# Six shifted copies of a transformed row: twelve transfers inside SBUF in place of a store to DRAM and a load

## The chip, the cores and the metric

The kernel runs on one core of one Trainium2 chip. The metric is the device time of one execution in microseconds (us). Times of runs of one kernel differ by about 0.2%.

The engines are called as in the profile: PE is TensorE (matmuls; PEld is its loading of weights), DVE is VectorE, ACT is ScalarE, POOL is GpSimd, and SP is SyncE, which here only issues DMAs. All DMAs run on 16 DMA engines. SBUF is the on-chip memory with 128 partitions, PSUM the memory that matmuls write to, DRAM the memory off the core.

## The reference

The input x has the shape (4, 512, 512, 16): four images of 512 x 512 pixels with 16 channels, float32. Two layers follow one another, each added to its input after a group normalization `_gn`:

```python
x = x + _L0_conv_ref(_gn(x), h0, numerators, denumerator)
x = x + _L1_conv_ref(_gn(x), kernel, bias, radius)
```

The first layer is a convolution by way of Fourier transforms. A filter of 16 x 16 channels is given as a quotient of two polynomials in two dimensions:

```python
H_truncated = rfft2(b, s=(512, 512)) / rfft2(a, s=(512, 512))
h_truncated = irfft2(H_truncated, s=(512, 512))
H = rfft2(h_truncated, s=(1024, 1024))
H_full = h0 + H[0]
X = rfft2(x, s=(1024, 1024), axes=(-3, -2))
Y = einsum('...hwi,ijhw->...hwj', X, H_full)
y = irfft2(Y, s=(1024, 1024), axes=(-3, -2))
return y[..., :512, :512, :]
```

So at every frequency a vector of 16 input channels is multiplied by a 16 x 16 matrix, for each of the four images. The second layer is a 3 x 3 convolution with a normalization by the norm of the input window, an arc cosine and a gate; it isn't touched here.

## The kernel before

`body` runs four stages after one another. `filter_phase` makes the spectrum of the filter along one axis and stores it to DRAM as `g_d`. `forward_phase` transforms the normalized image along the same axis and stores it as `x_d`. `conv_phase` does the other axis and the product of the channels, and stores `y_d`. `last_phase` transforms back and does the second layer. The change touches `conv_phase` alone.

`conv_phase` runs over 513 rows (frequencies of the first axis; the first row of all is split in two planes). The second axis has 512 points, which the kernel treats as 8 blocks of 64 points, each transformed to 128 frequencies; the convolution over whole blocks is what the shifted slots below are for. A row n goes through these steps:

- `load_x(n)` and `load_g(n)` bring the row of the image (128 partitions x 2 KB) and of the filter (128 x 8 KB) into SBUF, on SP's DMA queue.
- `x_part(n, b)` multiplies the image row by a Fourier matrix on PE, and `evict` copies the result from PSUM to slot 0 of `xe`. A row's `xe` is a tile of 128 partitions x 8 slots x 1024 floats (4 KB a slot and partition), with three buffers. The partition stands for a pair of a block and a channel: 8 blocks x 16 channels. A shift by one block is a shift by 16 partitions.
- `x_late(n)` makes on POOL a second version `xl` of slot 0, multiplied by complex factors `late`: four products into the scratch tile `u` (named xu in the profile, L807), one product into `xl` (L808) and one addition (L809).
- Slots 1 to 7 of `xe` hold slot 0 shifted by 16, 32, up to 112 partitions. The partitions that would come from beyond the end come from `xl`, from its start.
  - Slot 4, the shift by 64, is made by two copies on ACT in `half_shift` (L818): partitions 64 to 127 of slot 0 go to partitions 0 to 63, and partitions 0 to 63 of `xl` go to partitions 64 to 127.
  - For the six others, `store(0, ...)` and `store(1, ...)` in `x_late` write slot 0 from partition 16 on, and `xl` up to partition 111, one below the other to a DRAM buffer `xf_d` (L800, issued on POOL's queue). Then `load_xe` (L824, on SP's queue) reads it back with overlapping rows: one transfer for slots 1 to 3 and one for slots 5 to 7, each with 128 partitions x 3 slots x 4 KB. There are four DRAM buffers, used in turn.
- `g_part(n, j)` turns the filter row into its spectrum `gh` on PE (L838), with evictions on ACT and DVE.
- `mix(n, g)` does the product over the channels (L854): for each of 128 frequencies one matmul of `gh` with all eight slots of `xe`. It is the only reader of the slots other than slot 0 (and, with the change, of slot 4 as scratch).
- `over_q` and `over_g` transform the result `yf` back along this axis (PE L875 and L912, ACT L882, DVE L883 to L887, POOL L891 and L893), and the row goes to `y_d` by a DMA on POOL's queue (L923).

`step(n)` sets the program's order: it does `mix` for row n, `g_part` for row n+1, `over_q` for row n-1, `x_part`, `x_late` and `half_shift` for row n+2, `over_g` for row n-2, in four parts k = 0 to 3. Before the parts it loads x of row n+3, g of row n+2, and the shifted slots of row n+1. A planner orders the instructions of each engine from this program before the kernel runs, by its own costs, and sets the waits; an engine then runs its instructions in that fixed order. In the trace the order on ACT within a row is: evictions of part 0, one eviction of xe, the first copy of `half_shift`, evictions of part 1, the second copy of `half_shift`, evictions of part 2 and 3. PSUM has three banks for `pg`, two for `pm`, and three that `px`, `pz` and `py` share.

Of the kernel before, what the change touches and what calls it, by code (L numbers as in the profile page):

```python
# [40 lines left out]
F32 = mybir.dt.float32  # L41
# [5 lines left out]
P = 128  # L47
N = 512
B = 4
C = 16  # L50
S = 64
F = 128
# [4 lines left out]
XF = F * 2 * B  # L57
# [144 lines left out]
def bc(ap, axis, shape):  # L202
    return ap.unsqueeze(axis).to_broadcast(shape)
# [501 lines left out]
def conv_phase(tc, cst, g_d, x_d, y_d):  # L705
    nc = tc.nc
    with ExitStack() as ctx:
# [3 lines left out]
        xlp = ctx.enter_context(tc.tile_pool(name="h_xl", bufs=1))  # L711
# [10 lines left out]
        ig = load_const(nc, cp, cst, "ig").rearrange("p (s c n) -> p s c n", s=4, c=2)  # L722
        late = load_const(nc, cp, cst, "late").rearrange("p (v f) -> p v f", v=3)

        xf_d = [tc.dram_tile([16 * C, XF], F32, name=f"xf_d{n}") for n in range(4)]


        rows = [(0, 0, 0), (0, 0, 1)] + [(n // P, n % P, None) for n in range(1, N)]
        n_rows = len(rows)
        state = {}  # L730
        flip = [0]

        def evict(dst, src):
            flip[0] += 1
            if flip[0] % 3 == 0:
                nc.vector.tensor_copy(dst, src)  # L736
            else:
                nc.scalar.copy(dst, src)  # L738

        def load_g(n):  # L740
            rc, r, plane = rows[n]
            g = io.tile([P, C, 8 * C], F32, name="g")
            t, w = g.rearrange("p j x -> p (j x)"), C * 8 * C
            if plane is None:
                nc.sync.dma_start(out=t, in_=dram(g_d[rc], r, 0, [w, P], [1, w]))
            else:
                for to, at in ((0, (0, 96)[plane]), (64, (64, 32)[plane])):
                    nc.sync.dma_start(out=t[to : to + 32], in_=dram(g_d[rc], r, at * w, [w, 32], [1, w]))
                    nc.gpsimd.memset(t[to + 32 : to + 64], 0.0)
            state["g", n] = g  # L750

        def load_x(n):
            rc, r, plane = rows[n]
            x = io.tile([P, B, 8 * C], F32, name="x")
            t, w = x.rearrange("p b x -> p (b x)"), B * 8 * C
            if plane is None:
                nc.sync.dma_start(out=t, in_=dram(x_d[rc], r, 0, [w, P], [1, w]))
            else:
                nc.gpsimd.memset(t[S:], 0.0)
                nc.sync.dma_start(out=t[:S], in_=dram(x_d[rc], r, plane * S * w, [w, S], [1, w]))  # L760
            state["x", n] = x
# [16 lines left out]
        def x_part(n, b):  # L778

            if b == 0:  # L780

                state["xe", n] = xep.tile([P, 8, F, 2, 2, 2], F32, name="xe")
            if b % 2 == 0:
                state["px"] = ps_f.tile([P, 2, F, 2], F32, name="px", tag="full")
            px = state["px"]
            nc.tensor.matmul(px[:, b % 2].rearrange("p f c -> p (f c)"), state["x", n][:, b],
                             state["dfs", n], start=True, stop=True)
            if b % 2:
                evict(state["xe", n][:, 0, :, b // 2], px.rearrange("p k f c -> p f c k"))
            if b == B - 1:  # L790
                del state["x", n], state["dfs", n]

        def x_late(n):

            xe = state["xe", n][:, 0]
            fl = xe.rearrange("p f h c k -> p f (h c k)")

            def store(half, t):
                at = slice(C, P) if half == 0 else slice(0, P - C)
                nc.gpsimd.dma_start(out=xf_d[n % 4][half * P :, :][at], in_=t[at].rearrange("p f x -> p (f x)"))  # L800

            store(0, fl)
            xl = xlp.tile([P, F, 2, 2, 2], F32, name="xl")
            u = xlp.tile([P, F, 2, 2, 2], F32, name="xu")
            for c in range(2):
                for h in range(2):
                    nc.gpsimd.tensor_mul(u[:, :, h, c], xe[:, :, h, 1 - c], bc(late[:, 1 + c], 2, [P, F, 2]))  # L807
            nc.gpsimd.tensor_mul(xl.rearrange("p f h c k -> p f (h c k)"), fl, bc(late[:, 0], 2, [P, F, 8]))  # L808
            nc.gpsimd.tensor_add(xl.rearrange("p f h c k -> p (f h c k)"),  # L809
                                 xl.rearrange("p f h c k -> p (f h c k)"),  # L810
                                 u.rearrange("p f h c k -> p (f h c k)"))
            store(1, xl.rearrange("p f h c k -> p f (h c k)"))
            state["xl"] = xl

        def half_shift(n, half):

            dst, src = ((slice(0, 64), state["xe", n][64:, 0]), (slice(64, P), state["xl"][:64]))[half]
            nc.scalar.copy(state["xe", n][dst, 4].rearrange("p f h c k -> p (f h c k)"),  # L818
                           src.rearrange("p f h c k -> p (f h c k)"))

        def load_xe(n):
            src = xf_d[n % 4]
            for t in (1, 5):
                nc.sync.dma_start(  # L824
                    out=state["xe", n][:, t : t + 3].rearrange("p t f h c k -> p t (f h c k)"),
                    in_=bass.AP(tensor=src.tensor, offset=src.offset + t * C * XF,
                                ap=[[XF, P], [C * XF, 3], [1, XF]]),
                )

        def g_part(n, j):  # L830


            if j % 4 == 0:
                state["pg"] = [ps_g.tile([P, 4, F], F32, name=f"pg{c}", tag="pg") for c in range(2)]
            g, pg = state["g", n], state["pg"]
            for c in range(2):
                half = slice(64 * c, 64 * c + 64)
                nc.tensor.matmul(pg[c][:, j % 4], g[half, j], dg[half], start=True, stop=True)  # L838
            if j == 3:
                state["gh", n] = ghp.tile([P, F, 2, C], F32, name="gh")  # L840
            if j % 4 == 3:
                for c in range(2):
                    evict(state["gh", n][:, :, c, j - 3 : j + 1], pg[c].rearrange("p j f -> p f j"))
            if j == C - 1:
                del state["g", n]

        def mix(n, g):

            if g % 8 == 0:
                state["pm"] = ps_m.tile([P, 8, 8, 2 * B], F32, name="pm")  # L850
            xe, gh, pm = state["xe", n], state["gh", n], state["pm"]
            for q in range(4):
                f = g + 32 * q
                nc.tensor.matmul(  # L854
                    pm[32 * q : 32 * q + 32, g % 8], gh[:, f].rearrange("p c j -> p (c j)"),
                    xe[:, :, f].rearrange("p t h c k -> p t (h c k)"), start=True, stop=True,
                )
            if g == 7:

                state["y", n] = yp.tile([P, 16, 32, 4], F32, name="yf")  # L860
            if g % 8 == 7:
                evict(state["y", n][:, :, g - 7 : g + 1].rearrange("p t g x -> p g t x"),
                      pm.rearrange("p g t (h x) -> p g (t h) x", h=2))
            if g == 31:
                del state["xe", n], state["gh", n]
# [65 lines left out]
        def step(n):  # L931


            def row(k):
                return 0 <= n + k < n_rows

            if row(3):
                load_x(n + 3)
            if row(2):
                load_g(n + 2)  # L940
            if row(1):
                load_xe(n + 1)
            for k in range(4):
                if row(0):
                    for g in range(8):
                        mix(n, 8 * k + g)
                if row(1):
                    for j in range(4):
                        g_part(n + 1, 4 * k + j)
                if row(-1):  # L950
                    for t in range(4):
                        over_q(n - 1, 4 * k + t)
                if row(2) and k == 0:
                    for m in range(B):
                        x_part(n + 2, m)
                    x_late(n + 2)
                if row(2) and k >= 2:
                    half_shift(n + 2, k - 2)
                if row(3) and k == 2:
                    turn_x(n + 3)  # L960
                if row(-2) and k == 2:
                    for m in range(4):
                        over_g(n - 2, m)

        for n in range(-3, n_rows + 2):
            step(n)
# [479 lines left out]
```

## Time and profile before

| what | value |
|---|---|
| median of the three runs | 18372.5 us |
| the runs | 18348.46, 18387.49, 18372.5 us |
| the profiled execution | 18378.82 us |
| its span (first to last instruction) | 18377.0 us |
| mean granted PE clock | 0.939 of full speed |
| first and last copy of `half_shift` | 6426.3 and 15491.8 us |
| HBM read and written | 3030.71 and 1477.31 MB |

The profile is one execution. Its span is cut into 40 slices of 459 us; the slices that carry a digit of the busy share show the stages. Groups of instructions are named by line, engine, output and input, with a count, the total busy time and the mean of one. A list of waits gives for each waiting line the line that released it, the total of idle time, how often, and the longest. A DMA share of 1 is all 16 DMA engines busy; it can come out a little above 1 in a short stretch. A name in the profile is a tile's name: xe, xl, xu, gh, pm and pg are those of the text above.

In the trace of one row (9003 to 9020 us), the products of row n+2 on POOL run from 9007.5 to 15.3 us past 9000, the two copies of `half_shift` on ACT start at 9008.75 and 9015.31, the store of `xl` is issued at 9015.57, and the loads of the slots are issued at 9019.54 and 9020.54.

### The profile page before, as it was taken

Reading aid. Unit: us, or ns where it says so; the run is one execution under the profiler, and the core shown is the slowest. Engines: PE = TensorE matmul, PEld = TensorE weight load, DVE = VectorE, ACT = ScalarE, POOL = GpSimd, SP = SyncE. Lnnn points to the kernel's source line nnn. Section 1 sums busy time; section 2 is a strip of 40 time slices with the busy share of each in tenths; the row PEclk is TensorE's granted clock in tenths of the full one; section 3 lists DMA queues with packets and bytes.
Section 4 is the critical chain, followed back from the end, with each engine's and each line's share of the span. In section 5 each row is a group of like instructions: output and inputs, shape, how many; then the busy total and the mean of one; then the engine's idle time right before and its main releaser. Section 6 shows DMA issues by size and latency. Waiting matters only on the chain. (4 is left out here: it accounts for less than half of the span.)

```text
span 18377.0 us, 546088 instructions
## 1 busy us (share of the span) xinstructions
PE 16100.0 (88%) x233100; PEld 11615.5 (63%) x233100; DVE 11247.9 (61%) x23131; ACT 9599.6 (52%) x19919; POOL 10502.4 (57%) x10653
## 2 busy tenths in 40 slices
PE   7788888888889988888888888888888988988888
PEld 4444444444444467777777777777767776877777
DVE  8877777777833355555555555555555554246887
ACT  4556555555632255555555555555555554106788
POOL 5566666666621166666666666666666664026776
PEclk6888988888999999999999999999999999998999
DMA  4655555555676588888888888888888887795431
GB/s 123 201 162 165 162 165 162 164 163 161 167 221 184 167 319 320 318 321 324 316 321 318 319 325 323 325 325 323 323 323 314 325 320 289 257 324 192 160 129 69
DMA packets 2918877, 4543.47 MB, mean 247 GB/s; under 512 B 117634, under 2 KB 2086492, under 8 KB 2809694
## 3 DMA queue, kind: packets, MB, share of 16 engines
q1 hardware_dynamic: 2686254, 3768.39, 60.7%
q0 software_dynamic: 174896, 605.89, 8.7%
q10 hardware_dynamic: 55296, 134.24, 2.2%
q8 instruction: 1835, 30.06, 0.6%
q14 instruction: 596, 4.88, 0.1%
HBM read 3030.71 MB, written 1477.31 MB: 245 GB/s over the span
## 5 line engine op out<-in xcount | busy, mean ns | idle before, releaser
L838 PE MATMUL pg<-c_dg,g 64*128 64x128 f32 x32832 | 2836.9, 291 | 326.6 <-ACT gh L738 163.0
L854 PE MATMUL pm<-xe,gh 128*32 128x64 f32 x131328 | 2397.8, 222 | 587.8 <-issue 354.6
L854 PEld LDWEIGHTS pm<-xe,gh 128*32 128x32 f32 x131328 | 2011.9, 110 | 1165.3 <-issue 972.6
L838 PEld LDWEIGHTS pg<-c_dg,g 64*128 64x128 f32 x32832 | 2283.3, 190 | 670.4 <-issue 253.4
L456 PE MATMUL pt<-ev_in,c_todd 128*128 128x512 f32 x4096 | 2191.1, 681 | 350.4 <-ACT ot L461 323.9
L883 DVE TENSOR_TENSOR z<-zq,pz 128x256 f32<-128x256 f32 x2052 | 861.4, 420 | 2608.4 <-ACT zq L882 2531.1
L736 DVE COPY gh<-pg 128x512 f32<-128x512 f32 x2046 | 1410.1, 689 | 1312.1 <-PE pg L838 1308.2
L379 POOL TENSOR_TENSOR x<-ab,ab 128x512 f32<-128x512 f32 x1024 | 1561.1, 1524 | 1081.7 <-ACT ab L362 1029.0
L807 POOL TENSOR_TENSOR xu<-xe,c_late 128x256 f32<-128x256 f32 x2052 | 1389.5, 702 | 860.2 <-ACT xe L738 834.6
L377 DVE RECIPROCAL dn<-dn 128x256 f32<-128x256 f32 x1024 | 1781.8, 1740 | 0.0
L456 PEld LDWEIGHTS pt<-ev_in,c_todd 128*128 128x128 f32 x4096 | 792.4, 210 | 1483.1 <-issue 640.1
L738 ACT COPY yf<-pm 128x512 f32<-128x512 f32 x2046 | 1210.9, 592 | 924.0 <-PE pm L854 909.2
L362 ACT COPY ab<-pab 128x512 f32<-128x512 f32 x2048 | 1127.9, 617 | 858.7 <-PE pab L353 609.1
L818 ACT COPY xe<-xl 64x1024 f32<-64x1024 f32 x513 | 538.5, 1050 | 1872.5 <-POOL xl L809 1872.5
L738 ACT COPY gh<-pg 128x512 f32<-128x512 f32 x2058 | 1200.0, 583 | 398.4 <-PE pg L838 389.5
L875 PE MATMUL pz<-c_ident,yf 128*128 128x128 f32 x8208 | 1377.4, 291 | 30.3 <-issue 28.5
L404 PE MATMUL pg<-c_dinv,sp 64*128 64x128 f32 x16384 | 1192.7, 301 | 117.8 <-ACT sp L393 117.8
L404 PEld LDWEIGHTS pg<-c_dinv,sp 64*128 64x128 f32 x16384 | 1084.7, 209 | 313.2 <-PE pab L353 134.1
L376 DVE TENSOR_TENSOR m<-ab,ab 128x512 f32<-128x512 f32 x1024 | 1271.4, 1242 | 0.0
L809 POOL TENSOR_TENSOR xl<-xl,xu 128x1024 f32<-128x1024 f32 x513 | 1208.9, 2357 | 40.2
L383 POOL TENSOR_TENSOR m<-m 128x256 f32<-128x256 f32 x1024 | 747.0, 730 | 746.4 <-DVE m L376 746.2
L1289 PE MATMUL pc<-l_band,xn 128*128 128x160 f32 (+2 forms) x6144 | 1072.9, 333 | 53.7 <-DVE e_o L1344 53.5
(204 smaller groups left out, 31381.8 us busy)
## 6 DMA issues: line engine op xcount, KB each, us to landing
xe<-xf_d SPq DMA_DIRECT2D x1026, 1536.0 KB, 8.4
g<-g_d SPq DMA_DIRECT2D x511, 1024.0 KB, 9.8
g_d<-st SPq DMA_DIRECT2D x64, 4096.0 KB, 31.3
ev_in<-g_d SPq DMA_DIRECT2D x1024, 256.0 KB, 4.6
g_d<-ot SPq DMA_DIRECT2D x1024, 256.0 KB, 2.5
xf_d<-xe POOLq DMA_DIRECT2D x513, 448.0 KB, 8.3
xf_d<-xl POOLq DMA_DIRECT2D x513, 448.0 KB, 5.2
x_d<-xo SPq DMA_DIRECT2D x128, 1024.0 KB, 5.1
```

The costliest lines, as they stand in the source:

```text
L376: nc.vector.tensor_mul(w["m"], b, a)
L377: nc.vector.reciprocal(w["dn"], w["dn"])
L379: nc.gpsimd.tensor_mul(w["x"], b, a[:, :, ::-1])
L404: nc.tensor.matmul(pg[u][:, n, k].rearrange("p a x -> p (a x)"), w["sp"][q, k, c, :], dinv[q, 2 * kp + k, c, :], start=(c == 0), stop=(c = ...
L456: nc.tensor.matmul(pt, todd[:, c, kc, hh * P : hh * P + P], ev[:, kc, c], start=(kc == 0), stop=(kc == 1),)
L736: nc.vector.tensor_copy(dst, src)
L738: nc.scalar.copy(dst, src)
L807: nc.gpsimd.tensor_mul(u[:, :, h, c], xe[:, :, h, 1 - c], bc(late[:, 1 + c], 2, [P, F, 2]))
L809: nc.gpsimd.tensor_add(xl.rearrange("p f h c k -> p (f h c k)"), xl.rearrange("p f h c k -> p (f h c k)"), u.rearrange("p f h c k -> p (f ...
L838: nc.tensor.matmul(pg[c][:, j % 4], g[half, j], dg[half], start=True, stop=True)
L854: nc.tensor.matmul(pm[32 * q : 32 * q + 32, g % 8], gh[:, f].rearrange("p c j -> p (c j)"), xe[:, :, f].rearrange("p t h c k -> p t (h c k ...
L875: nc.tensor.transpose(pz[:, t % 4].rearrange("p v q x -> p (v q x)"), y[:, at].rearrange("p g x -> p (g x)"), ident)
```

## The change

`xf_d`, both stores and `load_xe` are taken out. A new function `shift` copies, for each of the six slots, the part that comes from slot 0 (half 0) and the part that comes from `xl` (half 1), each with one DMA from SBUF to SBUF on SP's queue: twelve a row, of 112, 96, 80, 48, 32 and 16 partitions in half 0, and of 16, 32, 48, 80, 96 and 112 in half 1, with 4 KB a partition. They stand in the program right before and after `x_late`, for row n+2, one row earlier than `load_xe` stood. `xl` has two buffers in place of one, and the scratch `u` is now slot 4 of the row's own `xe`, which `half_shift` writes over later.

```diff
-        xf_d = [tc.dram_tile([16 * C, XF], F32, name=f"xf_d{n}") for n in range(4)]
-
...
             xe = state["xe", n][:, 0]
             fl = xe.rearrange("p f h c k -> p f (h c k)")
 
-            def store(half, t):
-                at = slice(C, P) if half == 0 else slice(0, P - C)
-                nc.gpsimd.dma_start(out=xf_d[n % 4][half * P :, :][at], in_=t[at].rearrange("p f x -> p (f x)"))
-
-            store(0, fl)
-            xl = xlp.tile([P, F, 2, 2, 2], F32, name="xl")
-            u = xlp.tile([P, F, 2, 2, 2], F32, name="xu")
+            xl = xlp.tile([P, F, 2, 2, 2], F32, name="xl", bufs=2)
+            u = state["xe", n][:, 4]
...
-            store(1, xl.rearrange("p f h c k -> p f (h c k)"))
             state["xl"] = xl
...
-        def load_xe(n):
-            src = xf_d[n % 4]
-            for t in (1, 5):
-                nc.sync.dma_start(
-                    out=state["xe", n][:, t : t + 3].rearrange("p t f h c k -> p t (f h c k)"),
-                    in_=bass.AP(tensor=src.tensor, offset=src.offset + t * C * XF,
-                                ap=[[XF, P], [C * XF, 3], [1, XF]]),
-                )
+        def shift(n, half):
+
+            xe, src = state["xe", n], state["xl"] if half else state["xe", n][:, 0]
+            for t in (1, 2, 3, 5, 6, 7):
+                at = C * t
+                to, of = ((slice(0, P - at), slice(at, P)), (slice(P - at, P), slice(0, at)))[half]
+                nc.sync.dma_start(out=xe[to, t].rearrange("p f h c k -> p f (h c k)"),
+                                  in_=src[of].rearrange("p f h c k -> p f (h c k)"))
...
-            if row(1):
-                load_xe(n + 1)
...
                 if row(2) and k == 0:
                     for m in range(B):
                         x_part(n + 2, m)
+                    shift(n + 2, 0)
                     x_late(n + 2)
+                    shift(n + 2, 1)
```

More of the change, by code (lines that the diff above doesn't have):

```diff
@@ L819, in half_shift @@
                            src.rearrange("p f h c k -> p (f h c k)"))
-        def load_xe(n):
-            src = xf_d[n % 4]
-            for t in (1, 5):
-                nc.sync.dma_start(
-                    out=state["xe", n][:, t : t + 3].rearrange("p t f h c k -> p t (f h c k)"),
-                    in_=bass.AP(tensor=src.tensor, offset=src.offset + t * C * XF,
-                                ap=[[XF, P], [C * XF, 3], [1, XF]]),
-                )
+        def shift(n, half):
[3 more added lines that the diff above has]
+                to, of = ((slice(0, P - at), slice(at, P)), (slice(P - at, P), slice(0, at)))[half]
+                nc.sync.dma_start(out=xe[to, t].rearrange("p f h c k -> p (f h c k)"),
+                                  in_=src[of].rearrange("p f h c k -> p (f h c k)"))
         def g_part(n, j):
```

## The prediction

> **What bounds the kernel now.** I began with the page's busy shares and slices, to find the stage that the change touches, went on to the table of DMA issues, then to the list of waits of PE inside that stage, then to stretches of one microsecond, and last to the order of instructions within one row.
>
> ```profile
> PE 16100.0 (88%) x233100; PEld 11615.5 (63%) x233100; DVE 11247.9 (61%) x23131; ACT 9599.6 (52%) x19919; POOL 10502.4 (57%) x10653
> DMA  4655555555676588888888888888888887795431
> GB/s 123 201 162 165 162 165 162 164 163 161 167 221 184 167 319 320 318 321 324 316 321 318 319 325 323 325 325 323 323 323 314 325 320 289 257 324 192 160 129 69
> ```
>
> The flat run of twenty slices at about 320 GB/s is conv_phase, from about 6420 to 15530 us. Nothing outside it changes. Per row it moves:
>
> ```profile
> xe<-xf_d SPq DMA_DIRECT2D x1026, 1536.0 KB, 8.4
> g<-g_d SPq DMA_DIRECT2D x511, 1024.0 KB, 9.8
> xf_d<-xe POOLq DMA_DIRECT2D x513, 448.0 KB, 8.3
> xf_d<-xl POOLq DMA_DIRECT2D x513, 448.0 KB, 5.2
> x<-x_d SPq DMA_DIRECT2D x511, 256.0 KB, 12.1
> y_d<-yo POOLq DMA_DIRECT2D x511, 256.0 KB, 3.1
> ```
>
> Two loads of 1536 KB, two stores of 448 KB, g, x and y make 3.146 + 0.918 + 1.049 + 0.262 + 0.262 = 5.64 MB. Between 7000 and 15000 us there are 452.5 copies of each half shift, so a row takes 8000/452.5 = 17.68 us, and 5.64 MB in that is 319 GB/s, as the page shows. The DMA share there is 0.865 (seven stretches of 460 us lie between 0.86 and 0.88): 15.3 us of all 16 engines in each 17.68.
>
> PE is busy 0.89 of the same time, so it idles 1.97 us a row. Its waits in that stretch (waiting line, what released it, us in total, times, longest):
>
> ```profile
> PE pm L854 <- issue: 308.6, 302, 4.6
> PE pg L838 <- ACT gh L738: 137.5, 165, 3.7
> PE pg L838 <- issue: 134.9, 90, 3.0
> PE pm L854 <- DMA xe<-xf_d: 90.4, 66, 3.2
> PE pm L854 <- ACT zq L882: 52.5, 144, 0.6
> ```
>
> "Issue" is the largest: with the smaller ones on py, pz and px 503 us, 1.11 us a row, idling inside groups of equal matmuls where no operand is awaited. The list of the first 6000 us, at a DMA share near 0.56, has no such entry for PE. Two of them (9042 and 9048 us) fall where the DMA share is 1.00 or more. I read them as instructions arriving late behind data on the DMA engines; that is an inference. Next come 0.42 us a row behind ACT and 0.20 behind a late xe load. So PE is the nominal bound, and DMA, almost full, is what delays it.
>
> Within a row the engines alternate between full and nearly empty (us, then busy time and count of PE, PEld, DVE, ACT, POOL, then PE clock, DMA share, GB/s):
>
> ```profile
> 9018.00:9019.00 1.00, 1.00 (x15) 0.88 (x12) 0.90 (x4) 1.00 (x3) 0.48 (x1) 1.00 0.44 156
> 9024.00:9025.00 1.00, 1.00 (x39) 0.67 (x41) 0.93 (x5) 0.32 (x1) 0.60 (x1) 1.00 1.08 442
> ```
> ```profile
> 6418.00:6419.00 1.00, 0.00 (x0) 0.00 (x0) 0.00 (x0) 0.00 (x0) 0.91 (x1) 0.50 0.78 156
> 6419.00:6420.00 1.00, 0.00 (x0) 0.00 (x0) 0.00 (x0) 0.00 (x0) 0.00 (x0) 0.50 0.94 273
> 6420.00:6421.00 1.00, 0.00 (x0) 0.00 (x0) 0.31 (x1) 0.51 (x1) 0.00 (x0) 0.50 0.68 234
> 6421.00:6422.00 1.00, 0.72 (x2) 0.67 (x3) 0.42 (x2) 0.51 (x1) 0.00 (x0) 0.50 0.89 238
> ```
>
> These give prices in engine-us per MB (share x 16 / MB moved in 1 us). Loads over 128 partitions, at 9024: 1.08 x 16 / 0.442 = 39. The tail of the store from xl, 112 partitions, at 9018: 0.44 x 16 / 0.156 = 45. From 6418 to 6422 mostly the first g and x loads, on 32 and 64 partitions, are in flight: 3.29 x 16 / 0.901 = 58.
>
> **What it removes.** Both stores (0.918 MB) and the DRAM side of the loads. POOL loses two issues of 0.57 and 0.58 us a row; it has idle time in every row (1.65 us ahead of xu alone, 741.7/452), so the issues count only where they delay xl:
>
> ```profile
> 9008.75 1.04 ACT L818 COPY xe<-xe 64x1024 f32<-64x1024 f32 x1 [1.35 <-DVE xe L736]
> 9008.96 0.57 POOL L800 DMA_DIRECT2D xf_d<-xe  x1
> ...
> 9012.92 2.36 POOL L809 TENSOR_TENSOR xl<-xl,xu 128x1024 f32<-128x1024 f32 x1
> ...
> 9015.31 1.05 ACT L818 COPY xe<-xl 64x1024 f32<-64x1024 f32 x1 [3.75 <-POOL xl L809]
> ```
>
> The first store stands between two pairs of xu; without it, xl is done 0.66 us sooner (the 8.85 to 9.55 gap, less the usual 0.04). SP's wait for the store from xl, 5809.5/452 = 12.9 us a row, goes, and with it the dip seen at 9018; SP's wait held back only the g load behind it. The late loads go if the copies land sooner: they are issued a row earlier, so -0.20 us a row, -103 us.
>
> **What it adds.** On SP twelve issues replace two: at the load's median of 0.39 us, 4.7 us instead of 0.8. SP idles 12.9 us a row there, so I cost this at nothing; the longest issue at that line was 3.2 us, and twelve such would not fit a row. The first six wait for DVE's eviction of xe, the last six for xl at about 9014.6; behind them on SP stand the next x and g loads. g cannot start before about 9019.5, when its buffer comes free, and x has more than a row, so nothing is late. If the six were delayed past that, g_part in the next row would be next to wait, since g takes 9.8 us to land.
>
> PE's first mix of a row must now see twelve transfers, not two. Its queue has two semaphore instructions there, at 51 ns least; ten more would be 0.5 us, under the 2.1 us that the second one waits anyway. Nothing, or +260 us without that cover. Similar waits of 17 to 49 ns on ACT, DVE and POOL lie in their idle time.
>
> u moves into slot 4 of xe: same shape, and slot 0 of the same buffer has to be free by then in any case. The second xl buffer removes waits that sum to 3.2 us in the whole run. Both nothing.
>
> **What it moves.** Slot 4 is now scratch until the add at L809 has read it, so the first half shift, at 9008.75 now, cannot run before about 9014.6. ACT then owes two copies of 1.05 us where one stood; if they go back to back, the eviction behind them comes 1.05 - 0.66 = 0.39 us later, at most +200 us; if the second copy goes after the evictions, they come 0.66 us sooner, at most the 0.42 us that PE waits for ACT, -215 us. The order isn't visible in this trace. I take +200 where DMA doesn't bind; where it does, the wait is hidden by that.
>
> **The term that decides: 3.146 MB from SBUF to SBUF.** No row shows one. Lower bound, as cheap as a full load: 39 x 3.146 / 16 = 7.7 us. Upper bound, a narrow load and a store one after the other: 58 + 45 = 103, 20.3 us. Nearer rows lie inside: the narrow loads (58) have one end on few partitions, as the pieces of 16 to 48 have at both ends; a full load and a store in turn (39 + 45 = 84) pass SBUF twice, as every byte now does. I take their middle, 71: 14.0 us. To this come g, x and y, 1.573 MB at the row's mean price of 15.3 x 16 / 5.64 = 43.4: 4.3 us. Together 18.3 us. The fourteen stretches from 9004 to 9018 have a mean share of 0.98; at 0.97 a row takes 18.87 us. DMA becomes the bound: (18.87 - 17.68) x 513 = +610 us. Break-even is at 0.97 x 17.68 - 4.3 = 12.85 us, that is a price of 65.
>
> [...]
>
> **The sum.** Span 18377.0 + 610 = 18987; the execution is 18378.8, 1.8 over its span, and the median of the runs 18372.5, 6.3 below it: 18,980.
>
> **Rivals.**
> 1. DMA is relieved. At 39 the row needs 7.7 + 4.3 = 12.0 us, share 0.68. With issue waits of 0 at 0.56 and 1.11 at 0.865, a straight line gives 0.44 at 0.68: -0.67, and -0.20 for late loads: -0.87 x 513 = -446, about 17,930 (17,700 to 18,250). For it: 442 GB/s in loads, and 16% fewer bytes. Against: the narrow rows.
> 2. ACT becomes the wait. At 58 DMA needs 15.8 us, as now; the late loads go (-103) and the first half shift behind xl costs +200: 18,470. It decides from a price below 65 if the two copies run back to back. For it: ACT already stands 3.75 us at 9015.31, with evictions behind. Against: the 0.66 us.
> 3. It is hidden: the same price, with those terms cancelling: 18,372.
> 4. Each byte costs two passes or more: at 84, 16.5 + 4.3 = 20.8, a row of 21.5, +1940: 20,310, and 22,300 at 103. For it: pieces of 16 partitions. [...]
>
> **How the numbers follow.** Forecast 0.36 (own range 18,450 to 20,300); rival 1 0.28; rival 2 0.17, of which 0.02 faster by the kinder order; rival 3 0.07; rival 4 0.12. About 0.2% is what a measurement of this kernel can tell from no change. Faster 0.30, same 0.07, slower 0.63. The range, 17,850 to 20,400, leaves out the lower part of rival 1 and most of rival 4.
>
> **What would show it.** Right: GB/s in conv_phase falls to about 250 with the DMA share at 0.95 or more, and PE's wait at L854 goes to the shift's DMA. Wrong in price: a share below 0.8 with the row shorter. Wrong in the moves: PE's waits for ACT gh grow while DMA doesn't bind; or SP's issues last microseconds each and g comes late. The forecast falls if the transfers cost less than 65 engine-us per MB.

## The result and the profile after

The changed kernel takes 19735.47 us (median of 4 runs, 19731.41 to 19779.49) against 18360.48 us of the kernel before on the same chip: ratio 1.0756, 95% interval 1.0731 to 1.0781, slower by some 1,375 us. The forecast was +610 us.

From the page of the kernel after, the engines' busy time and the rows of the 40 slices (slices of 493 us; conv_phase is the flat run of twenty-one, some 6400 to 16800 us):

```profile
PE 16659.6 (84%) x233100; PEld 11858.7 (60%) x233100; DVE 10996.2 (56%) x23131; ACT 9666.4 (49%) x19919; POOL 9962.0 (50%) x9627
DMA  4755555655765999999999999999999999687441
GB/s 128 203 160 162 160 160 163 172 159 163 215 190 165 231 234 235 233 237 237 234 230 232 234 232 236 234 237 235 237 237 233 238 233 232 223 321 235 155 136 69
```

Where the page before had an 8 and 320 GB/s, it now has a 9 and 235 GB/s: fewer bytes a second, and fuller DMA engines. The stretch of 8000 us (time, then busy time and count of PE, PEld, DVE, ACT, POOL, PE clock, DMA share, GB/s) of the kernel before and then of the kernel after, and PE's waits in it in the kernel after:

```profile
7400.00:15400.00 8000.00, 7143.10 (x162715) 5706.77 (x162712) 4344.55 (x11749) 4211.88 (x7681) 5083.14 (x4970) 0.98 0.87 321
```
```profile
7400.00:15400.00 8000.00, 6630.49 (x141458) 5142.29 (x141459) 3585.18 (x10217) 3711.13 (x6679) 4006.03 (x3537) 0.93 0.99 234
```
```profile
PE pm L846 <- issue: 861.3, 493, 5.9
PE pg L830 <- issue: 214.3, 113, 6.6
PE pg L830 <- ACT gh L736: 78.3, 88, 2.6
PE pz L867 <- DVE z L879: 72.2, 123, 1.1
PE px L784 <- DVE z L879: 48.6, 216, 0.6
PE py L904 <- issue: 43.9, 31, 3.7
PE pz L867 <- issue: 28.4, 18, 3.8
PE px L784 <- issue: 9.5, 6, 2.9
```

The stretch holds 393 rows (2358 copies from xe at L819, six a row), so a row takes 20.36 us in place of 17.68, and 2.68 x 513 = 1,375 us, the whole loss. Waits on "issue" are 861.3 + 214.3 + 43.9 + 28.4 + 9.5 = 1157 us, 2.94 us a row against 1.11 before. The mix at L846 almost never waits for the copies as such: the trace puts 0.7 us of its waiting in the whole stretch down to them. In all PE idles 3.48 us a row against 1.90, and that is 1.6 of the 2.68 us. The other 1.07 us is PE's own busy time, 16.87 us a row against 15.80, at a mean granted clock of 0.93 against 0.98 (15.80 x 0.98 / 0.93 = 16.65).

The queue table of the kernel after (queue, packets, MB, share of 16 engines' span) and, below it, that of the kernel before:

```profile
q1 hardware_dynamic: 2768334, 3768.72, 74.7%
...
q8 instruction: 1843, 30.20, 0.7%
```
```profile
q1 hardware_dynamic: 2686254, 3768.39, 60.7%
```

q1 is SP's queue. It moves the same bytes in both kernels, for 0.747 x 16 x 19730 = 235,800 engine-us in place of 0.607 x 16 x 18377 = 178,500. q8 carries instructions, by its count PE's: 1843 packets of 16 KB for PE's 471,755 instructions, one for every 256.

That gives a test of the reading of "issue" as late instructions, in the trace's packets and starts. In the stretch of the kernel after, PE has 749 pauses of more than 0.3 us between matmuls of one line. 82% of them, 1137 us in all, end 1.15 to 1.85 us after a packet of q8 has landed; of random moments 10% would. Of the distances from one pause to the next, 72% are a multiple of 256 instructions, to within 8; by chance 7% would be. In g1 (below), where hardly any other wait is left, it is 100% and 99.8% of 625 pauses. So PE stands there for its next 256 instructions. The median packet of q8 took 1.28 us in the kernel after and 0.96 us before.

The timeline of SP within one row of the kernel after (start, duration, line, transfer, count):

```profile
9027.34 2.37 SPq L755 DMA_DIRECT2D x<-x_d  x1
9029.80 1.29 SPq L743 DMA_DIRECT2D g<-g_d  x1
9031.30 8.72 SPq L819 DMA_DIRECT2D xe<-xe  x6
9040.12 1.26 SPq L819 DMA_DIRECT2D xe<-xl  x2
```

Six issues take 8.72 us where the prediction had 0.39 each. Over the stretch the median of one is 0.75 us from xe and 0.53 from xl, the longest 4.4. SP has the time: it still waits 1302 us of the stretch, 3.3 us a row, for DVE's eviction of xe ahead of the first copy, and PE's list has no wait for g.

### The profile page after: what moved, and what is told of

Its sections match the earlier page's. It is cut to its first block, busy times and chain, and to the rows that moved or that the text cites. A ratio compares the mean times of both kernels' runs of the same rounds, so it can differ in the third digit from the quotient of the medians.

```text
span 19730.0 us, 555296 instructions
## 1 busy us (share of the span) xinstructions
PE 16659.6 (84%) x233100; PEld 11858.7 (60%) x233100; DVE 10996.2 (56%) x23131; ACT 9666.4 (49%) x19919; POOL 9962.0 (50%) x9627
## 3 DMA queue, kind: packets, MB, share of 16 engines
q8 instruction: 1843, 30.20, 0.7%
## 5 line engine op out<-in xcount | busy, mean ns | idle before, releaser
L846 PE MATMUL pm<-xe,gh 128*32 128x64 f32 x131328 | 2659.9, 229 | 1115.3 <-issue 1106.6
L846 PEld LDWEIGHTS pm<-xe,gh 128*32 128x32 f32 x131328 | 2164.3, 115 | 1826.4 <-issue 1707.4
L830 PE MATMUL pg<-c_dg,g 64*128 64x128 f32 x32832 | 2768.1, 303 | 407.7 <-issue 285.2
L915 POOL DMA_DIRECT2D y_d<-yo x511 | 296.5, 580 | 3127.2 <-ACT yo L736 3086.5
L800 POOL TENSOR_TENSOR xe<-xe,c_late 128x256 f32<-128x256 f32 x2052 | 1441.7, 727 | 594.1 <-DVE xe L734 289.7
L810 ACT COPY xe<-xe 64x1024 f32<-64x1024 f32 x513 | 536.1, 1045 | 1795.2 <-POOL xl L802 1794.5
L883 POOL TENSOR_TENSOR zd<-z 128x512 f32<-128x512 f32 x513 | 652.4, 1272 | 1434.3 <-DVE z L875 1434.1
L784 PE MATMUL px<-dfs_n,x 128*128 128x256 f32 x4104 | 1218.1, 417 | 92.5 <-DVE z L879 61.8
```

The costliest lines, as they stand in the source:

```text
L846: nc.tensor.matmul(pm[32 * q : 32 * q + 32, g % 8], gh[:, f].rearrange("p c j -> p (c j)"), xe[:, :, f].rearrange("p t h c k -> p t (h c k ...
```

## The experiments

All 18 kernels stand against runs of the kernel before on their own chip. "Rows" is the time of a row in the stretch from 7400 to 15400 us, "share" the DMA share there, "price" the engine-us per MB of the six slots' 1614 MB: the busy time of q1 less that of e6, which has no copies, divided by those bytes. For the kernel after that is (235,800 - 114,700) / 1614 = 75.0; for the kernel before it is the price of the loads from DRAM alone, 39.5. The subtraction takes the other transfers of q1, g and x among them, to cost what they cost in e6; what they lose to fuller engines is counted as the copies'.

| run | what it is | median us | ratio, 95% | row us | share | price |
|---|---|---|---|---|---|---|
| e1 | after, no copies | 18999.07 | 1.0369 [1.0348, 1.0389] | 18.9 | 0.27 | - |
| e2 | after, six unshifted copies of 128 partitions | 19176.32 | 1.0465 [1.0444, 1.0486] | 19.4 | 0.67 | 39.2 |
| e3 | after, the twelve pieces unshifted | 19491.73 | 1.0638 [1.0609, 1.0666] | 19.9 | 0.97 | 70.8 |
| e4 | before, with u in slot 4 and two xl | 18996.29 | 1.0375 [1.0352, 1.0398] | 19.0 | 0.81 | 38.1 |
| e5 | after, u in slot 7 | 19834.31 | 1.0799 [1.0780, 1.0817] | 20.5 | 0.98 | 74.3 |
| e6 | e1 with u a tile of its own | 18252.0 | 0.9938 [0.9920, 0.9956] | 17.5 | 0.29 | - |
| e7 | e2 with u a tile of its own | 18257.84 | 0.9941 [0.9923, 0.9959] | 17.5 | 0.75 | 40.6 |
| e8 | before, second half shift on POOL | 18389.34 | 1.0008 [0.9998, 1.0017] | 17.7 | 0.87 | 39.6 |
| e9 | e7 in twelve copies of 128 x 2 KB | 18378.18 | 1.0026 [1.0015, 1.0036] | 17.7 | 0.76 | 42.1 |
| e10 | e7 as 64 + 64 partitions | 19300.13 | 1.0526 [1.0504, 1.0548] | 19.6 | 0.92 | 64.5 |
| e11 | e8 with the stores on SP | 18683.62 | 1.0191 [1.0174, 1.0208] | 18.3 | 0.84 | - |
| e12 | e7 as 112 + 16 partitions | 19245.83 | 1.0497 [1.0476, 1.0518] | 19.4 | 0.85 | 57.3 |
| f1 | after's pieces, engine order held | 19689.71 | 1.0741 [1.0725, 1.0757] | 20.3 | 0.99 | 75.0 |
| f2 | f1 with full-width copies | 18407.28 | 1.0045 [1.0030, 1.0060] | 17.8 | 0.75 | 40.7 |
| f3 | before, engine order held | 19592.62 | 1.0691 [1.0675, 1.0706] | 20.1 | 0.76 | 38.2 |
| f4 | f3, second half shift late | 18407.4 | 1.0042 [1.0028, 1.0056] | 17.8 | 0.87 | 39.4 |
| g1 | before, transform early, order held | 18306.84 | 0.9957 [0.9940, 0.9973] | 17.5 | 0.87 | 39.1 |
| g2 | g1, POOL not held | 18314.77 | 0.9949 [0.9932, 0.9966] | 17.4 | 0.87 | 39.0 |

### The change taken apart: e1 to e4

The edits, in turn: e1 (no copies; the mix reads slot 0 eight times), e2, e3 and, in the kernel before, e4.

```diff
-            for t in (1, 2, 3, 5, 6, 7):
...
+            return
...
-                    xe[:, :, f].rearrange("p t h c k -> p t (h c k)"), start=True, stop=True,
+                    xe[:, 0, f].rearrange("p h c k -> p (h c k)").unsqueeze(1).to_broadcast([P, 8, 2 * B]),
```
```diff
-                nc.sync.dma_start(out=xe[to, t].rearrange("p f h c k -> p (f h c k)"),
-                                  in_=src[of].rearrange("p f h c k -> p (f h c k)"))
+                nc.sync.dma_start(out=xe[:, t].rearrange("p f h c k -> p f (h c k)"),
+                                  in_=xe[:, 0].rearrange("p f h c k -> p f (h c k)"))
```
```diff
-                                  in_=src[of].rearrange("p f h c k -> p (f h c k)"))
+                                  in_=src[to].rearrange("p f h c k -> p (f h c k)"))
```
```diff
-            xl = xlp.tile([P, F, 2, 2, 2], F32, name="xl")
-            u = xlp.tile([P, F, 2, 2, 2], F32, name="xu")
+            xl = xlp.tile([P, F, 2, 2, 2], F32, name="xl", bufs=2)
+            u = state["xe", n][:, 4]
```

> The changed kernel without its twelve copies; the product reads slot 0 eight times instead of slots 0 to 7, with as many matmuls, so its output is not the convolution's. Theory (the copies fill the DMA engines, and PE loses its time to instructions that come late behind them): DMA keeps only g, x and y, about 4.3 us of a row, PE's issue waits fall below 0.2 us a row from 2.9, a row takes 16 to 17 us, 17,500 to 18,100 us. Rival (the moved half shift and the planner's new order on ACT and POOL cost the time): it stays above 19,000 us.

> Same 3.146 MB a row from SBUF to SBUF, but as six copies of all 128 partitions of slot 0 onto slots 1 to 3 and 5 to 7 without a shift, so the output is not the convolution's. Theory A (the dear thing is the shape: few partitions, or source and destination in different partitions): 39 to 45 engine-us per MB, DMA share below 0.8, 17,600 to 18,300 us. Rival B (SBUF to SBUF is dear by itself, because every byte passes SBUF twice): about 79 engine-us per MB as in the changed kernel, share above 0.95, 19,500 to 19,900 us. Rival C (a fixed cost for each transfer): half of the excess goes, about 19,000 us.

> The same twelve pieces of 16 to 112 partitions as in the changed kernel, but each read from the partitions it is written to, so the output is not the convolution's. If few partitions are the dear thing, or SBUF to SBUF itself, or the count of transfers: 19,400 to 19,900 us as in the changed kernel. If the shift is (source and destination partitions apart): 17,700 to 18,500 us.

> The kernel before with its DRAM round trip, but with the scratch in slot 4 of xe and two buffers for xl, so that the first half shift has to wait for the addition on POOL. Prediction's bounds for the move: -215 to +200 us, 18,150 to 18,570 us. If the moves are what makes the changed kernel slow, above 19,000 us.

Measured: e1 lost 3.7% although it moves nothing, and e4, which leaves the transfers as they were, lost as much, +675 us. So the move of the scratch is a cost of its own, which the prediction had bounded at +200 us. The stretch and PE's longest wait in e1, two of e4's waits, then ACT in one row of e4 (start, duration, operation, idle before it):

```profile
7400.00:15400.00 8000.00, 7192.39 (x152410) 5801.70 (x152412) 4031.62 (x11010) 3954.97 (x7196) 4303.33 (x3810) 0.91 0.27 86
```
```profile
PE pg L826 <- ACT gh L736: 674.0, 423, 2.1
```
```profile
PE pm L854 <- ACT zq L882: 488.9, 322, 2.1
PE pm L854 <- issue: 463.2, 358, 3.7
```
```profile
9002.86 1.04 ACT L818 COPY xe<-xe 64x1024 f32<-64x1024 f32 x1 [2.99 <-POOL xl L809]
9003.81 0.57 ACT L738 COPY yf<-pm 128x512 f32<-128x512 f32 x1
9004.39 1.05 ACT L818 COPY xe<-xl 64x1024 f32<-64x1024 f32 x1
9005.47 0.59 ACT L738 COPY gh<-pg 128x512 f32<-128x512 f32 x1
9005.95 0.37 ACT L882 COPY zq<-pz 128x256 f32<-128x256 f32 x1
```

Both copies of the half shift now stand behind xl with one eviction between them, and gh and zq, which PE waits for, come after both: 1.6 us a row in e1 (674.0/423), 1.16 in e4 (488.9/422). That wait is not the whole price, though. In e1 it takes the place of others: PE idles 1.91 us a row in all, as before (1.90). What grew is PE's busy time, 17.00 us a row against 15.80, as the granted clock fell from 0.98 to 0.91. In e4 PE idles 0.96 us a row more and is busy 0.3 more, at 0.95. The copies themselves tell the rest: full width costs 39.2, the pieces 70.8 unshifted and 75.0 shifted. The shape costs (31.6 more), and the shift little (4.2 more). These runs don't yet say which of the two makes the kernel after slow: e2, with the move and cheap copies, already has 4.65% of its 7.56%.

### The move undone: e5, and the old place of u without narrow copies: e6, e7

e5, in the kernel after (the copies of slot 7 are issued last):

```diff
-            u = state["xe", n][:, 4]
+            u = state["xe", n][:, 7]
```

e6 and e7 are e1 and e2 with

```diff
-            xl = xlp.tile([P, F, 2, 2, 2], F32, name="xl", bufs=2)
-            u = state["xe", n][:, 4]
+            xl = xlp.tile([P, F, 2, 2, 2], F32, name="xl")
+            u = xlp.tile([P, F, 2, 2, 2], F32, name="xu")
```

> The changed kernel with the scratch in slot 7 instead of slot 4, so that the first half shift is free of POOL again as in the kernel before; only the first copy of slot 7 (16 partitions) now waits for the addition. Theory D (the DMA engines, 0.98 busy, set the row, and the half shift is hidden behind them): 19,500 to 19,800 us, hardly below the changed kernel. Theory S (the half shift and the copies add up): the 1.3 us a row of e4_moves_alone go, about 19,050 us.

> As e1_no_copies (no copies; the product reads slot 0 eight times, so the output is not the convolution's), but with the scratch in a tile of its own as before. If the half shift behind the addition is what kept e1_no_copies at 18,999 us: 17,700 to 18,000 us, and PE's wait for ACT's eviction of gh back from 1.6 to about 0.4 us a row. If it is something else on ACT or POOL: within 100 us of 18,999.

> As e2_full_width (six unshifted copies of 128 partitions, output not the convolution's), but with the scratch in a tile of its own. Shape theory: copies at the price of loads (44 engine-us per MB) leave DMA at a share near 0.75 and PE with few issue waits; without the moved half shift the row is shorter than before: 17,700 to 18,150 us. If SBUF to SBUF were dear in itself: above 18,400 us.

With the half shift free again, e5 is no faster than the kernel after (1.0799 and 1.0756), while without narrow copies the same freedom is worth 1.0369 - 0.9938 (e1, e6) and 1.0465 - 0.9941 (e2, e7), 4 to 5%. So here the move costs much where the DMA engines have room (shares of 0.27 to 0.75), and nothing where they have none (0.98 and 0.99): it is hidden behind them.

e6 and e7 also show what the best relief of DMA is worth with the engines in this order: 0.6%, some 110 us. The stretch and PE's waits in e6:

```profile
7400.00:15400.00 8000.00, 7109.66 (x164942) 5709.42 (x164938) 4299.44 (x11942) 4226.76 (x7783) 4654.15 (x4123) 1.00 0.29 93
```
```profile
PE pm L842 <- DVE gh L734: 586.8, 457, 1.3
PE pg L826 <- ACT gh L736: 273.3, 424, 0.7
PE pm L842 <- issue: 15.2, 48, 0.8
```

At a share of 0.29 the waits on issue are all but gone, and the evictions of gh have taken their place: 860 us in 457 rows, 1.88 us a row, as much as PE idled before (850.2 us in 452 rows, 1.88). What the row gained is in PE's busy time, 15.56 us against 15.80, at a granted clock of 1.00 against 0.98. The same holds between e6 and e1: PE idles 1.95 and 1.91 us a row, and all of the 1.4 us that the move costs there is busy time, 15.56 us at a clock of 1.00 against 17.00 at 0.91. In e7 the first of these waits appears as "issue" (581.2 us, about once a row, never over 1.3 us); I take it for the same wait under another name: in the rows from 9000 us on it stands at the same place, behind two matmuls of pg and ahead of a group of the mix, for 1.24 us in e7 and 1.28 in e6. It is not the wait for instructions: of e7's pauses between matmuls of one line, 14% end at the distance from a q8 packet given above, against 11% of random moments.

### Number, height and balance: e8 to e12

e9 and e10 put these in the place of e7's loop body; e12 is e10 with 112 in place of 64:

```diff
+                for w in (slice(0, F // 2), slice(F // 2, F)):
+                    nc.sync.dma_start(out=xe[:, t, w].rearrange("p f h c k -> p f (h c k)"),
+                                      in_=xe[:, 0, w].rearrange("p f h c k -> p f (h c k)"))
```
```diff
+                for w in (slice(0, 64), slice(64, P)):
+                    nc.sync.dma_start(out=xe[w, t].rearrange("p f h c k -> p f (h c k)"),
+                                      in_=xe[w, 0].rearrange("p f h c k -> p f (h c k)"))
```

e8, in the kernel before, has the first of these edits, e11 both:

```diff
-            nc.scalar.copy(state["xe", n][dst, 4].rearrange("p f h c k -> p (f h c k)"),
-                           src.rearrange("p f h c k -> p (f h c k)"))
+            copy = nc.gpsimd.tensor_copy if half else nc.scalar.copy
+            copy(state["xe", n][dst, 4].rearrange("p f h c k -> p (f h c k)"),
+                 src.rearrange("p f h c k -> p (f h c k)"))
...
-                nc.gpsimd.dma_start(out=xf_d[n % 4][half * P :, :][at], in_=t[at].rearrange("p f x -> p (f x)"))
+                nc.sync.dma_start(out=xf_d[n % 4][half * P :, :][at], in_=t[at].rearrange("p f x -> p (f x)"))
```

> The kernel before with the second half shift on POOL instead of ACT, so that ACT no longer stands 3.65 us a row for xl. If ACT's stand is worth the 0.42 us a row that PE waits for ACT: 18,100 to 18,250 us. If POOL's copy delays the store of xl and so the loads behind it: 18,400 to 18,800 us.

> As e7_full_width_old_order, but each of the six copies cut in two along the free dimension: twelve transfers of 128 partitions x 2 KB, same bytes (output not the convolution's). If the count of transfers made the copies dear: 19,300 to 19,900 us and a DMA share above 0.95. If the partitions do: the price stays near 45 engine-us per MB, 18,200 to 18,350 us.

> As e7_full_width_old_order, but each copy cut in two halves of 64 partitions, unshifted: twelve transfers of 64 x 4 KB, same bytes (output not the convolution's). [...] If the count alone matters: as e9. If pieces overlap and fill each other's gaps: 18,200 to 18,600 us.

> e8_before_halfshift_on_pool with both stores to DRAM issued from SP instead of POOL; it computes the convolution. In e8 PE's wait for late loads had taken the place of its wait for ACT (0.59 us a row at L855). If POOL's two issues of 0.57 us hold up xl: 18,050 to 18,250 us. If the landing of the store (about 6 us) is what is late: 18,300 to 18,450 us; if SP's order puts a store behind a waiting load: above 18,500 us.

> As e10_two_halves, but each copy cut into 112 and 16 partitions, unshifted (output not the convolution's). [...] If the narrow piece of 16 is what is dear, not the half: above 19,300 us.

Twelve transfers of full width (e9) cost 42.1 each MB and 0.9% over e7: the number of transfers isn't it. Two halves cost 64.5, 112 + 16 partitions 57.3: the same bytes are dearer when a transfer has only part of the partitions. How dear doesn't follow from that alone, since e3's uneven pairs, at 70.8, lie above both. The times of e10 and e12 are no measure of that, however. At shares of 0.92 and 0.85, PE waits for ACT gh (580.7 and 672.9 us) and little for issue (201 and 75 us): the planner had put these kernels in another order. That is why the next runs hold the order fixed.

In the kernel before, e8 takes ACT's stand ahead of the second copy away and gains nothing; e11 then takes the store off POOL and loses 1.9%. PE's wait that grew, in e8 and then in e11:

```profile
PE pm L855 <- DMA xe<-xf_d: 266.8, 138, 5.4
```
```profile
PE pg L839 <- DMA g<-g_d: 488.3, 236, 4.5
```

The late loads went from 0.20 to 0.59 us a row as the wait for ACT went; with the stores on SP, g stands in SP's queue behind a store that waits 5.6 us a row for xl.

### The same order on every engine, and only the copies' shape different: f1 and f2

f1 is the kernel after with u in slot 7 and the program's order held on PE, ACT, DVE and POOL (an engine then takes its instructions as `step` writes them, with the half shifts in parts 0 and 1 and `turn_x` in part 1); f2 is f1 with each pair of pieces replaced by two copies of 128 partitions x 2 KB, unshifted.

```diff
+        held = InOrder(tc, nc.tensor, nc.vector, nc.scalar, nc.gpsimd)
         for n in range(-3, n_rows + 2):
-            step(n)
+            with held:
+                step(n)
```
```diff
-                at = C * t
-                to, of = ((slice(0, P - at), slice(at, P)), (slice(P - at, P), slice(0, at)))[half]
-                nc.sync.dma_start(out=xe[to, t].rearrange("p f h c k -> p (f h c k)"),
-                                  in_=src[of].rearrange("p f h c k -> p (f h c k)"))
+                w = slice(half * F // 2, (half + 1) * F // 2)
+                nc.sync.dma_start(out=xe[:, t, w].rearrange("p f h c k -> p f (h c k)"),
+                                  in_=xe[:, 0, w].rearrange("p f h c k -> p f (h c k)"))
```

> The changed kernel with scratch in slot 7, and the order of PE, ACT, DVE and POOL held to the program's in conv_phase, with the half shifts and turn_x placed where the kernel before runs them; it computes the convolution. If the narrow copies bound the row through the DMA engines: 19,500 to 19,900 us and a DMA share above 0.95. If the planner's other order of PE, ACT and DVE (which came with narrow copies in e5, e10 and e12) is the cause: below 18,700 us.

> The same held order as f1_pieces_held_order, instruction by instruction on PE, ACT, DVE and POOL, but twelve unshifted copies of 128 partitions x 2 KB (output not the convolution's). DMA theory: 18,250 to 18,500 us, as e9_twelve_full_width. Order theory: within 200 us of f1.

The stretch and PE's first two waits, of f1 and then of f2:

```profile
7400.00:15400.00 8000.00, 6498.55 (x141748) 5182.21 (x141745) 3814.50 (x10241) 3696.63 (x6692) 3967.67 (x3546) 0.92 0.99 235
```
```profile
PE pm L846 <- issue: 880.2, 468, 5.8
PE pg L830 <- issue: 237.3, 116, 6.2
```
```profile
7400.00:15400.00 8000.00, 7046.34 (x161642) 5665.22 (x161640) 4292.13 (x11675) 4131.48 (x7634) 4538.89 (x4042) 0.97 0.75 268
```
```profile
PE pg L829 <- ACT gh L736: 470.6, 375, 1.7
PE pm L845 <- ACT zq L873: 339.2, 426, 0.8
PE pm L845 <- issue: 107.3, 85, 2.1
```

Same engine order, same bytes, same number of transfers, 1,282 us apart. With pieces the share is 0.99 and PE loses 3.1 us a row on issue (1228 us with the smaller ones, 394 rows); at full width 0.75 and 0.27 us. PE's busy time differs too, 16.49 us a row against 15.69, at 0.92 against 0.97. f2 also leaves out the shift, and its last six copies read slot 0 in place of xl; but the shift is worth 4 of the 34 engine-us per MB between them (e3), and in f2 SP's queue still stands for xl in every row (1281.5 us in 449). This settles the cause: the pieces' price fills the DMA engines, and PE pays by "issue" and by a lower clock.

### Can the kernel before be beaten? f3, f4, g1, g2

f3 was meant as a control, the kernel before held in the order of f1; f4 puts the second half shift into part 3; g1 moves the transform and the four xu products to the start of the step, the first store behind the products, the half shifts into parts 0 and 2, and `turn_x` into part 1; g2 is g1 without POOL held.

```diff
             for k in range(4):
+                if row(2) and k == 0:
+                    for m in range(B):
+                        x_part(n + 2, m)
+                    x_late(n + 2)
                 if row(0):
...
-                if row(2) and k >= 2:
-                    half_shift(n + 2, k - 2)
+                if row(2) and k in (0, 2):
+                    half_shift(n + 2, k // 2)
```

> The kernel before with its round trip through DRAM, in the same held order: what the held order alone is worth. If it stands for the planner's order of before: 18,250 to 18,500 us.

> As f3_round_trip_held_order, but with the second half shift on ACT after the evictions of part 2 and 3, where xl is long done, so that ACT never stands for xl. As e8 showed that late loads take the place of this wait: within 100 us of f3. If ACT's stand did cost: 200 us below f3.

> The kernel before with its store and load through DRAM, PE, ACT, DVE and POOL held to the program's order, and the transform of row n+2 and its four xu products moved to the start of the step, so that the half shift and the store from xl come early. Theory of balance: the stand of ACT ahead of the half shift (0.42 us a row at PE) and the late loads (0.20 us a row) both go, the waits on issue stay at about 1.1 us a row while the DMA share is near 0.87: 18,000 to 18,250, below both kernels. Rival, the waits only move: another edge (g behind its buffer, PE's mix behind the evictions of px) takes their place, 18,300 to 18,500. Above 18,500 if the evictions of px now stand in front of mix's and PE waits for a bank in every row.

> The same, with PE, ACT and DVE held and POOL left to the planner. Theory of balance: as the run beside it, 18,000 to 18,250. If POOL's order was what kept xl late, this run is faster than the one beside it by 0.2 us a row or more (100 us); if the planner puts the store ahead of the xu products again, it is slower, 18,500 or more with PE waiting for ACT gh.

f3 is a failed control: the held order put the first store ahead of all xu products on POOL, where it waits for DVE's eviction; xl comes later and ACT stands 2221.1 us ahead of the half shift, 5.6 us a row, with PE waiting 716.2 us for gh behind it. PE's busy time is 17.10 us a row there, at a clock of 0.88. It shows only how steep that chain is. In f4 the late half takes that away, and the late loads come in its place: 467.8 us, 1.04 a row. PE's waits in g1:

```profile
PE pm L854 <- issue: 630.6, 511, 4.6
PE pg L838 <- issue: 182.3, 118, 4.6
PE pg L838 <- DMA g<-g_d: 56.9, 45, 2.2
...
PE pm L854 <- DMA xe<-xf_d: 18.1, 14, 1.8
```

Here both go: no wait for ACT of any size, the late loads down from 89.8 to 18.1 us, ACT's stand for xl from 1644.2 to 45.5. What is left is issue, 1.9 us a row in place of 1.11, and 833 of its 867 us stand at the packets of q8. The gain is 0.4% (g1) and 0.5% (g2), both intervals below 1: 18,307 and 18,315 us against 18,401 on that chip. That is a version faster than both kernels, by about the 0.6% that e6 gets from having no copies at all, and less than the 18,000 to 18,250 expected. POOL's order makes no difference that these runs can tell.

## Why the prediction was right in direction and wrong in size

- **The mechanism** was right: "DMA becomes the bound". GB/s about 250 with a share of 0.95 or more was forecast; it is 234 with 0.99. f1 and f2 show it as the cause.
- **The failed step is the sum of the DMA time, "I take their middle, 71: 14.0 us", with the 4.3 us for g, x and y: "Together 18.3 us."** Measured: 0.99 x 16 x 20.36 = 322 engine-us a row, 20.2 us. The copies cost 75.0, 14.75 us; that leaves 86 engine-us, 5.4 us, for g, x and y. So the guess from far rows was 0.75 us short, and the term that looked safe 1.1 us. That 71 came so near 75.0 is in part luck: of the two rows it lies between, the 84 stood for bytes that "pass SBUF twice", and e7's copies, which read SBUF and write it, cost 40.6 at full width; few partitions, the reason behind the 58, is what the runs bear out (42.1 on 128, 64.5 on 64, twelve transfers each). The 43.4 was a mean over a row whose cheap half the change removes: at the 39.5 of the loads, 3.146 MB take 124 of the 245 engine-us, and the 2.49 MB left cost 48.4 each. By that alone g, x and y take 76 engine-us, 4.8 us; without copies (e6) they take 0.29 x 16 x 17.5 = 81, with the engines full 86. A row of 20.36 us in place of 18.87, times 513, is 764 us; the prediction was 755 us short.
- **The move**: "I take +200 where DMA doesn't bind; where it does, the wait is hidden by that." Hidden it is (e5). The bound was wrong: 790 us between e1 and e6, 960 between e2 and e7 by their ratios. It counted one late eviction by 0.39 us and took the rest of the order as fixed. The new dependency moved more than that, as e4's ACT timeline shows, and the sum held PE's busy time fixed: between e6 and e1, and between e7 and e2, PE's idle time is the same to 0.04 us a row, and the loss is busy time at a lower clock (1.00 to 0.91 and 1.00 to 0.89). How much of it is the planner's new order on the other engines wasn't taken apart.
- **Removed late loads, POOL's issues, twelve waits at PE, the second xl**: with DMA as the bound none of them shows. "PE's wait at L854 goes to the shift's DMA" was wrong: PE hardly waits for the copies' data (0.7 us at the mix), it runs short of instructions. A misreading besides: PE idled 1.90 us a row before (858 us in 452.5 rows), not 1.97; nothing rests on it.
- **SP's issues** are longer than costed (0.53 to 0.75 us at the median, 8.72 us for six in the row shown), and g isn't late for it, as forecast.
- **Rival 1** had its price of 39 right for full width (39.2 in e2, 40.6 in e7, 40.7 in f2) and its size wrong: 17,930 was made from waits that vanish. e7 has that price and gains 108 us, since the evictions of gh take over. **Rival 2's** mechanism is real (PE waits 674.0 us of the stretch for ACT's gh in e1, 714.4 in e2) and bigger than priced, but it isn't what the kernel after shows, where PE waits 78.3 us for it and 1157 on issue. **Rival 4's** price of 84 and more was too high: it is 75.0.

## What to carry to other kernels

When a transfer is replaced, price what remains by its own rows, not by a mean that holds the removed part; and price a copy within SBUF by the partitions of each single transfer, not by its bytes, which cost 39.2 to 75.0 engine-us per MB here. Where DMA engines are nearly full, the loss need not appear as a wait for data: at a share of 0.99, PE waited 0.7 us for the copies at the mix and 1157 us on issue. Read PE's busy time and its granted clock beside its waits: a change can leave the idle time as it was and still lose 4% (e6 to e1). A scratch that moves into a buffer with other writers adds an edge to the order, and the whole order behind it must be read again; a wait removed from a balanced loop tells little until one sees which wait is next (in e8, late loads of 0.59 us a row in place of 0.20).

## What the runs showed of the hardware

- Full-width copies within SBUF cost what loads from DRAM cost here: 40.6 (e7) and 39.5 (before) engine-us per MB.
- The same bytes cost 42.1 in twelve full-width transfers (e9), 57.3 as 112 + 16 partitions (e12), 64.5 as 64 + 64 (e10), 70.8 as the six uneven pairs (e3), 75.0 when these are shifted (the kernel after). Halves cost 1.59 times the six full-width copies (64.5/40.6), and 1.53 times the same number of transfers (64.5/42.1). Why the uneven pairs cost more than 64 + 64 was not tried by itself.
- PE's waits on issue, in us a row: 0.1 at a share of 0.27 (e1), 0.27 at 0.75 (f2), 2.6 at 0.97 (e3), 2.9 and 3.1 at 0.99 (after, f1). The mean share doesn't fix them: 0.18 in e12 at 0.85, 0.49 in e10 at 0.92, 1.5 in e4 at 0.81, 1.9 in g1 at 0.87. PE's instructions come in packets of 16 KB, one for 256 instructions, and the pauses stand at these (all 625 in g1, 82% of 749 in the kernel after). What decides whether a packet comes in time at a given share stays open.
- PE's busy time of a row goes with the granted clock: 15.56 us at 1.00 (e6), 15.80 at 0.98 (before), 16.87 at 0.93 (after), 17.00 at 0.91 (e1), 17.42 at 0.89 (e2). The trace has the clock at half for 4 of the 8000 us in e6 and for 1452 in e1, though PE idles as long in both; e6 has its idle time in two pauses a row, of 1.28 and 0.64 us in the mean, e1 mostly in one of 1.6. Whether the longer pause is what lowers the clock was not tried.
